# Moving the scatters of a second graph's edges between stages of a GNN and mixture-of-experts kernel

## The chip, the cores and the metric

The kernel runs on one core of a Trainium2 chip. It is one launch that computes eight stages. The metric is the device time of an execution in microseconds; the median of ten runs is given, and one profiled execution beside it. The engines are named as the profile names them: PE (TensorE, with PEld for its weight loads), DVE (VectorE), ACT (ScalarE), POOL (GpSimd) and SP (SyncE, which here issues most transfers). A name with a q behind it (SPq, POOLq) is the engine's sequencer.

## What is computed

Four graph rounds alternate with four mixtures of experts over 3125 nodes of 256 features; each reads the layer norm of x and adds its result to x.

```python
edge_index = jnp.stack([src, dst])                       # 50000 edges
x = x + _L0_gnn_ref(_layernorm(x), edge_weight, src, dst)        # round one: weighted sum over edges
x = x + _L0_ffn_ref(_layernorm(x), ...)                          # mixture one: top 2 of 8, relu, 512 hidden
x = x + _L1_gnn_ref(_layernorm(x), edge_index, ...)              # round two: two attention layers
x = x + _L1_ffn_ref(_layernorm(x), ...)                          # mixture two: top 2 of 8, gelu, 256 hidden
x = x + _L2_gnn_ref(_layernorm(x), edge_index, edge_weight, ...) # round three: normalised convolution
x = x + _L2_ffn_ref(_layernorm(x), ..., L2_ffn_edge_index)       # mixture three, routed by attention
x = x + _L3_gnn_ref(_layernorm(x), edge_index, ...)              # round four
x = x + _L3_ffn_ref(_layernorm(x), ...)                          # mixture four
```

Mixture three is the one that uses the other graph. Its routing scores come from an attention over 65536 edges of their own plus one loop per node:

```python
src = jnp.concatenate([edge_index[0], loops])
dst = jnp.concatenate([edge_index[1], loops])
e = leaky_relu(a_src[src] + a_dst[dst], 0.2)
ee = jnp.exp(e - segment_max(e, dst)[dst])
alpha = ee / (segment_sum(ee, dst)[dst] + 1e-16)
agg = segment_sum(h[src] * alpha[:, :, None], dst) + b_gat
```

To work on these edges in dense tiles, the kernel first sorts them by the block of 128 nodes that their destination lies in.

## The kernel before

The nodes are padded to 25 tiles of 128 (T = 25, P = 128), and x stays in SBUF as the tile X for the whole program.

**The other graph's scatters.** `own_places` computes for each of the 65536 edges a packed record (os_rec, 128 x 512) and the place in a DRAM table (os_at) at which it belongs. `own_send` (L1822) writes them: each call issues the next n of 512 columns, one indirect transfer on POOL for each (L1826), 128 records of one word. With no n it issues all that are left. Its second argument names an instruction that the scatters wait for; this only spreads them out in time. `settle` (L1836) reads one word of the table back, a transfer on SP that waits for the scatters issued so far; it stands ahead of each branch of the program. `own_load` (L1840) reads the finished table into SBUF (L1866, L1868) and decodes it (L1872 to L1885), and `own_order` (L1887, tiles oo_y and oo_h) sorts the edges of a block; both belong to round three.

The 512 are issued as follows: 21 in `rank_edges` (3 x 7) and 40 before the main loop of round one (5 x 8); 200 in its first 100 steps, two a step, and 12 in its last 25 (`src % 2`); 84 in the first mixture's 28 chunks (send=3); 36 in round two, at the end of its first layer (`tail`, 4 x 9); 98 in the second mixture's 28 chunks (send=3, more=2, thus 3 and 4 in turn); 21 at its end.

**Round one** (`r0_gnn`, L1482) runs 5 x 25 steps: five groups of destination tiles g, and in each all 25 source tiles. A step builds one-hot matrices on DVE (r_hs L1544, r_hd L1549), multiplies them on PE into a PSUM tile r_pw, copies that to SBUF on ACT (r_wt, L1557: the instruction `done` that a step's scatters wait for) and applies it to x on PE (L1521). Beside the steps of the first four groups the buckets of the next group are filled (`fill_bucket`: bf_h, bf_rh L1473, bf_hr, bf_ps on DVE, ACT and PE).

**Routing of a mixture.** In the last group of a round, as soon as five tiles of x are final, `mix_step` routes them: centred on ACT or DVE (gh_xn; ACT L191 in round one), squared, normalised, multiplied with the gate, top 2 picked on DVE, places computed (gd_at, L861). `mix_send` (L869) then scatters the ten batches (five tiles, two choices) from gh_xn on POOL into the DRAM regions of the experts. The tile gh_xn has two buffers. POOL, like each engine, runs what it is given in order, so L869 comes after all L1826 issued before it.

**The mixture** (`gated`) works in chunks of 256 rows of one expert: transfers in on SP (gx_xs, gx_w), transposes and two products on PE, the activation on ACT (gx_h, L1005; the last one of a chunk is what that chunk's scatters wait for), results out (ff_results). The next round begins with gathers of these results on POOL (gb_y, L360), which DVE adds to X (L1035).

**Round two** (`r1_gnn`) runs two attention layers. In each, POOL gathers rows for the edges (ad_rows, L360), and PE, DVE and ACT work on them. `tail` is called four times, twice in each of the last two blocks of the first layer; POOL has the last two calls' scatters just ahead of the second layer's first gathers.

The order of the instructions on each engine is set by a scheduler, except that from the first mixture to the second (`middle`, L2421) POOL's order is that of the text.

Of the kernel before, what the change touches and what calls it, by code (L numbers as in the profile page):

```python
# [27 lines left out]
AF = mybir.ActivationFunctionType  # L28
# [7 lines left out]
T = 25  # L36
# [27 lines left out]
class Net:  # L64
# [972 lines left out]
    def r0_ffn(self):  # L1037
        with ExitStack() as ctx:
            m = self.mix_whole(ctx, "L0_ffn_Wg", ("L0_ffn_bg", "L0_ffn_bias"), 8)
            self.sort_dst_end()  # L1040
            self.gated(m, "L0_ffn_W1", "L0_ffn_b1", "L0_ffn_W2", "L0_ffn_b2", AF.Relu)
# [20 lines left out]
    def r1_ffn(self):  # L1062
        with ExitStack() as ctx:
            m = self.mix_whole(ctx, "L1_ffn_router_w", (), 8, probs=True, transpose=True, add=True)
            self.gated(m, "L1_ffn_w1", "L1_ffn_b1", "L1_ffn_w2", "L1_ffn_b2", AF.Gelu)
# [149 lines left out]
class Fast(Net):  # L1215
# [266 lines left out]
    def r0_gnn(self):  # L1482
# [9 lines left out]
        G = 5  # L1492
        self.mix_way = ExitStack()
        m = self.mix = self.mix_start(self.mix_way, "L0_ffn_Wg", ("L0_ffn_bg", "L0_ffn_bias"), 8, act=True)
        with ExitStack() as ctx:
            pool = ctx.enter_context(tc.tile_pool(name="r0", bufs=1))
            lp = ctx.enter_context(tc.tile_pool(name="ln", bufs=1))
            bp = ctx.enter_context(tc.tile_pool(name="r0_b", bufs=2))
            hp = ctx.enter_context(tc.tile_pool(name="r0_h", bufs=3))
            psb = ctx.enter_context(tc.tile_pool(name="r0_pb", bufs=1, space=PSUM))  # L1500
            psw = ctx.enter_context(tc.tile_pool(name="r0_pw", bufs=2, space=PSUM))
            psa = ctx.enter_context(tc.tile_pool(name="r0_pa", bufs=2, space=PSUM))
            xn = pool.tile([P, T, D + 1], F32, name="r0_xn")
            nc.vector.memset(xn[:, :, D:], 1.0)
            iota1 = pool.tile([P, P], F32, name="r0_iota1")
            nc.vector.tensor_scalar_add(iota1, self.iota, 1.0)
            degs = pool.tile([P, T, T // G], F32, name="r0_degs")
            f5 = self.fill_fields(pool)
            for g in range(0, T, TG):
                self.norm_group(lp, xn[:, g:g + TG, 0:D], g, act=g // TG % 2 == 1)  # L1510

            wp = ctx.enter_context(tc.tile_pool(name="r0_w", bufs=2))

            psm = ctx.enter_context(tc.tile_pool(name="r0_pm", bufs=1, space=PSUM))
            self.mix_open(m, ctx, lambda: psb.tile([P, 512], F32, name="bf_ps"),
                          lambda: psm.tile([P, 80], F32, name="gh_ps"))

            def apply(g, src, wt):
                pa = psa.tile([P, D + 1], F32, name="r0_pa")
                for i in range(G):  # L1520
                    nc.tensor.matmul(pa, wt[:, i, :], xn[:, g * G + i, :], start=i == 0, stop=i == G - 1)  # L1521
                nc.vector.tensor_add(self.X[:, src, :], self.X[:, src, :], pa[:, 0:D])
                nc.scalar.copy(degs[:, src, g:g + 1], pa[:, D:D + 1])
                if g == T // G - 1:

                    self.mix_send(m, 2)
                    for _ in range(1 if src < T - 2 else 2):
                        self.mix_step(m, src + 1)


            for d in range(G):
                for _ in self.fill_bucket((bp, psb), f5, d):
                    pass
                self.own_send(8, self.filled)
            last = None
            for g in range(T // G):
                ds = slice(g * G, g * G + G)
                for src in range(T):
                    if g + 1 < T // G:
                        if src % G == 0:  # L1540
                            fill = self.fill_bucket((bp, psb), f5, (g + 1) * G + src // G)
                        next(fill, None)
                    hs = hp.tile([P, G, P], F32, name="r0_hs")
                    nc.vector.tensor_tensor(hs, self.iota[:, None, :].to_broadcast([P, G, P]),  # L1544
                                            s.bsrc[:, ds, src, None].to_broadcast([P, G, P]), OP.is_equal)
                    hd = hp.tile([P, G, P], F32, name="r0_hd")
                    for i in range(G):
                        d = g * G + i
                        nc.vector.tensor_scalar(hd[:, i, :], iota1, s.bdst[:, d, src:src + 1], s.bw[:, d, src:src + 1],  # L1549
                                                op0=OP.is_equal, op1=OP.mult)  # L1550
                    pw = psw.tile([P, G, P], F32, name="r0_pw")
                    for i in range(G):
                        nc.tensor.matmul(pw[:, i, :], hd[:, i, :], hs[:, i, :], start=True, stop=True)
                    if src % G == 0:
                        wide = wp.tile([P, G, G, P], F32, name="r0_wt")
                    wt = wide[:, src % G]
                    done = nc.scalar.copy(wt, pw)  # L1557
                    if src % G == G - 1:
                        nc.sync.dma_start(self.mats[:, src - G + 1:src + 1, ds, :], wide)
                    if last:  # L1560
                        apply(*last)
                    last = (g, src, wt)
                    self.own_send(2 if g < T // G - 1 else src % 2, done)
            apply(*last)
            self.mix_rest(m)
            nc.vector.tensor_reduce(self.deg, degs, AX.X, OP.add)
# [778 lines left out]
    def r1_gnn(self):  # L2345
# [5 lines left out]
        with tc.tile_pool(name="r1", bufs=1) as pool, tc.tile_pool(name="r1_ps", bufs=1, space=PSUM) as psp:  # L2351
# [38 lines left out]
                    self.mix_step(m, b + 1)  # L2390

            def tail(i):
                self.own_send(9, i)

            def rest(i):
                self.mix_send(m)

            self.attend(self.d, 64, rows[0], ad[0], sf[0], to_second, tail=tail)
            only.close()
            with ExitStack() as way:  # L2400
# [7 lines left out]


    def r0_ffn(self):  # L2410
        self.gated(self.mix, "L0_ffn_W1", "L0_ffn_b1", "L0_ffn_W2", "L0_ffn_b2", AF.Relu, beside=self.fill_edges, send=3, tail=False)

    def r1_ffn(self):
        self.gated(self.mix, "L1_ffn_w1", "L1_ffn_b1", "L1_ffn_w2", "L1_ffn_b2", AF.Gelu, send=3, more=2, tail=False)
        self.own_send()

    def r3_ffn(self):
# [415 lines left out]
```

## Time and profile before

| | us |
|---|---|
| median of ten runs | 5641.38 |
| lowest, highest | 5632.95, 5648.07 |
| the profiled execution | 5649.52 |
| its span | 5647.6 |
| PE busy | 3628.6 (64%) |
| DVE busy | 2849.8 (50%) |
| ACT busy | 2165.2 (38%) |
| POOL busy | 2107.0 (37%), 2107 instructions |

The stages in the span of the profiled execution, read from the first and last instructions of their own tiles, with the busy time in each:

| stage | from to | PE | DVE | ACT | POOL |
|---|---|---|---|---|---|
| setup, sorting of the first graph | 0-200 | 33.3 | 160.9 | 50.4 | 35.0 |
| round one, first group | 200-346 | 101.5 | 119.9 | 92.6 | 118.9 |
| round one, up to the last group | 346-608 | 261.8 | 219.5 | 159.1 | 152.8 |
| round one, last group, and routing | 608-778 | 126.5 | 112.7 | 70.8 | 62.7 |
| first mixture | 778-998 | 213.8 | 49.1 | 55.0 | 81.6 |
| round two | 998-2815 | 790.7 | 825.7 | 812.7 | 969.5 |
| second mixture | 2815-2998 | 135.7 | 42.6 | 28.4 | 95.8 |
| round three, its start | 2998-3104 | 27.0 | 57.8 | 11.1 | 85.4 |
| the rest | 3104-5647 | 1938.5 | 1261.7 | 885.1 | 505.4 |

A stage in which one engine is busy nearly all the time is bound by that engine; where none is, some wait sets the pace. In the lines of the profile, the bracket at the end of a timeline row gives the engine's idle time before the instruction and what ended it, and "issue" means that nothing in the profile held it.

### The profile page before, as it was taken

Reading aid. Unit: us, or ns where it says so; the run is one execution under the profiler, and the core shown is the slowest. Engines: PE = TensorE matmul, PEld = TensorE weight load, DVE = VectorE, ACT = ScalarE, POOL = GpSimd, SP = SyncE. Lnnn points to the kernel's source line nnn. Section 1 sums busy time; section 2 is a strip of 40 time slices with the busy share of each in tenths; the row PEclk is TensorE's granted clock in tenths of the full one; section 3 lists DMA queues with packets and bytes.
Section 4 is the critical chain, followed back from the end, with each engine's and each line's share of the span. In section 5 each row is a group of like instructions: output and inputs, shape, how many; then the busy total and the mean of one; then the engine's idle time right before and its main releaser. Section 6 shows DMA issues by size and latency. Waiting matters only on the chain. (4 is left out here: it accounts for less than half of the span.)

```text
span 5647.6 us, 66173 instructions
## 1 busy us (share of the span) xinstructions
PE 3628.6 (64%) x20909; PEld 2868.9 (51%) x20909; DVE 2849.8 (50%) x9396; ACT 2165.2 (38%) x5957; POOL 2107.0 (37%) x2107
## 2 busy tenths in 40 slices
PE   1499979324555324444583887554666699997994
PEld 1389868223333213333362776432433488886883
DVE  7978731434444325455524786524545788422112
ACT  2556432134554335445411797311222443111221
POOL 0765433555555455555357000255554000011003
PEclk9699979656666656666696998776887799997997
DMA  1722247333333133333162222201111011233554
GB/s 50 234 88 94 101 158 225 102 98 95 106 98 101 48 94 99 96 95 97 60 200 81 105 94 83 58 18 26 22 22 26 8 58 65 83 107 126 189 193 143
DMA packets 329438, 543.00 MB, mean 96 GB/s; under 512 B 69070, under 2 KB 242002, under 8 KB 325872
## 3 DMA queue, kind: packets, MB, share of 16 engines
q1 hardware_dynamic: 213430, 354.48, 18.6%
q0 software_dynamic: 84032, 154.27, 10.5%
q10 hardware_dynamic: 31610, 29.84, 1.6%
q8 instruction: 173, 2.83, 0.2%
q14 instruction: 193, 1.58, 0.1%
HBM read 393.49 MB, written 145.37 MB: 95 GB/s over the span
## 5 line engine op out<-in xcount | busy, mean ns | idle before, releaser
L360 POOL DMA_INDIRECT ad_rows<-r_rows,fa_gi x832 | 829.9, 997 | 614.8 <-PE ad_acc L2223 325.0
L1826 POOL DMA_INDIRECT os_table<-os_rec,os_at x512 | 548.7, 1072 | 631.3 <-ACT gx_h L1005 185.1
L360 POOL DMA_INDIRECT ad_rows<-q_rows,own_gi x416 | 400.3, 962 | 864.3 <-DVE ad_hb L2104 508.2
L2213 ACT ACTIVATE ad_rows<-ad_rows 128x64 f32<-128x64 f32 x2544 | 633.6, 335 | 90.7 <-issue 88.1
L2223 PE MATMUL ad_acc<-ad_rows,ad_hd 128*128 128x260 f32 x1664 | 601.9, 524 | 31.7 <-ACT ad_rows L2213 22.7
L2223 PEld LDWEIGHTS ad_acc<-ad_rows,ad_hd 128*128 128x128 f32 x1664 | 419.4, 266 | 121.6 <-ACT ad_rows L2213 29.0
L1654 PE MATMUL r_pa<-r_xs,r_cnt 128*128 128x257 bf16 (+1 forms) x3750 | 458.5, 276 | 9.2 <-issue 8.9
L869 POOL DMA_INDIRECT regions<-gh_xn,gd_at x150 | 148.1, 987 | 836.0 <-PE r_pa L1654 544.8
L1005 ACT ACTIVATE gx_h<-gx_pa,gx_bias 128x256 f32<-128x256 f32 x392 | 184.8, 473 | 603.5 <-PE gx_pa L1004 514.1
L1654 PEld LDWEIGHTS <-r_cnt 128*128 128x128 bf16 x3750 | 364.3, 99 | 64.3 <-issue 13.8
L974 PE MATMUL gx_po<-gx_w,gx_h 128*128 128x256 f32 x1568 | 374.7, 385 | 17.5 <-ACT gx_h L1005 14.1
L1004 PE MATMUL gx_pa<-gx_xt,gx_w 128*128 128x256 f32 x1568 | 370.6, 392 | 14.4 <-DVE gx_xt L999 8.7
L976 DVE TENSOR_TENSOR gx_ys<-gx_po,gx_b 128x256 f32<-128x256 f32 x168 | 70.8, 423 | 578.7 <-PE gx_po L974 495.0
L1004 PEld LDWEIGHTS gx_pa<-gx_xt,gx_w 128*128 128x128 f32 x1568 | 299.1, 195 | 80.3 <-DVE gx_xt L999 21.1
L360 POOL DMA_INDIRECT gb_y<-ff_results,gd_at x150 | 155.2, 1035 | 486.6 <-SPq L126 437.7
L2112 ACT CAST ad_hd<-ad_hb 128x2176 f32<-128x2176 bf16 (+1 forms) x50 | 98.3, 1967 | 608.8 <-PE ad_acc L2223 441.4
L974 PEld LDWEIGHTS gx_po<-gx_w,gx_h 128*128 128x128 f32 x1568 | 293.5, 193 | 60.3 <-ACT gx_h L1005 17.8
L2126 PE MATMUL ad_pt<-ident,ad_e 128*4 128x128 f32 x75 | 26.1, 348 | 453.1 <-DVE ad_F L2120 203.1
L1521 PE MATMUL r_pa<-r_xn,r_wt 128*128 128x257 f32 x1250 | 302.3, 387 | 19.8 <-ACT r_wt L1557 18.2
L2600 PE MATMUL ss_sum<-r_xw,ss_wt 128*128 128x256 f32 x1250 | 289.9, 394 | 6.2 <-DMA ss_wt<-mats 6.2
L2600 PEld LDWEIGHTS ss_sum<-r_xw,ss_wt 128*128 128x128 f32 x1250 | 245.4, 198 | 41.7 <-issue 6.6
L2182 PE MATMUL ad_px<-ad_nb,ad_hT 128*128 128x24 bf16 x1248 | 45.3, 179 | 333.2 <-DVE ad_nb L1420 234.8
(573 smaller groups left out, 7180.9 us busy)
## 6 DMA issues: line engine op xcount, KB each, us to landing
gx_w<-in_L_ffn_W SPq DMA_DIRECT2D x56, 1024.0 KB
mats<-r_wt SPq DMA_DIRECT2D x25, 1600.0 KB
ss_wt<-mats SPq DMA_DIRECT2D x25, 1600.0 KB
gx_w<-in_L_ffn_W SPq DMA_DIRECT2D x56, 512.0 KB
regions<-zero SPq DMA_DIRECT2D x26, 1024.0 KB
ad_rb<-fa_relT SPq DMA_DIRECT2D x48, 544.0 KB
gx_xs<-regions SPq DMA_DIRECT2D x84, 256.0 KB
ff_results<-gx_ys ACTq DMA_DIRECT2D x84, 256.0 KB
```

What stands on the lines that cost most here:

```text
L360: return self.nc.gpsimd.indirect_dma_start(out=out, out_offset=None, in_=table[:, :], in_offset=bass.IndirectOffsetOnAxis(ap=idx, axis=0))
L869: ins = nc.gpsimd.indirect_dma_start(out=self.regions[:, :], out_offset=bass.IndirectOffsetOnAxis(ap=m.at[i][:, t:t + 1], axis=0), in_=x, ...
L974: nc.tensor.matmul(po, h[:, f, j * P:(j + 1) * P], w2s[:, f, :], start=f == 0, stop=f == FC - 1)
L1004: nc.tensor.matmul(ps, w1s[:, c, f * P:(f + 1) * P], xt[:, c, :], start=c == 0, stop=c == DC - 1)
L1005: done = nc.scalar.activation(h[:, f, :], ps, act, bias=bias1[:, f, k:k + 1])
L1521: nc.tensor.matmul(pa, wt[:, i, :], xn[:, g * G + i, :], start=i == 0, stop=i == G - 1)
L1654: nc.tensor.matmul(pa[:, 0:n], c[:, u, :], xs[i][:, u, j, 0:n], start=u == 0 and j == 0, stop=u == T - 1 and j == 2)
L1826: i = nc.gpsimd.indirect_dma_start(out=s.table[:, :], out_offset=bass.IndirectOffsetOnAxis(ap=s.at[:, c:c + 1], axis=0), in_=s.rec[:, c, : ...
L2112: nc.scalar.copy(x.hd[:, :x.kb, :], x.hb[:, :x.kb, :])
L2213: i = nc.scalar.activation(v, v, AF.Copy, scale=x.rt[:, k, W4 + h:W4 + h + 1])
L2223: nc.tensor.matmul(x.acc, lhs[:, k, :], rhs[:, k, :], start=i == 0, stop=i == x.kb - 1)
L2600: nc.tensor.matmul(sums[t], wt[:, d, :], xw[:, d, :], start=d == 0, stop=d == T - 1)
```

## The change

Four numbers change. The scatters of the first 100 steps of round one go from two to three a step; `tail` issues 7 and not 9; the first mixture issues four a chunk and not three; the second mixture's calls ask for one a chunk, and find none left, and so does the call behind it.

```diff
@@ r0_gnn
-                    self.own_send(2 if g < T // G - 1 else src % 2, done)
+                    self.own_send(3 if g < T // G - 1 else src % 2, done)
@@ r1_gnn
             def tail(i):
-                self.own_send(9, i)
+                self.own_send(7, i)
@@ r0_ffn
-        self.gated(self.mix, "L0_ffn_W1", "L0_ffn_b1", "L0_ffn_W2", "L0_ffn_b2", AF.Relu, beside=self.fill_edges, send=3, tail=False)
+        self.gated(self.mix, "L0_ffn_W1", "L0_ffn_b1", "L0_ffn_W2", "L0_ffn_b2", AF.Relu, beside=self.fill_edges, send=4, tail=False)
@@ r1_ffn
-        self.gated(self.mix, "L1_ffn_w1", "L1_ffn_b1", "L1_ffn_w2", "L1_ffn_b2", AF.Gelu, send=3, more=2, tail=False)
+        self.gated(self.mix, "L1_ffn_w1", "L1_ffn_b1", "L1_ffn_w2", "L1_ffn_b2", AF.Gelu, send=1, tail=False)
         self.own_send()
```

| where | scatters before | after |
|---|---|---|
| `rank_edges` | 21 | 21 |
| round one, ahead of its steps | 40 | 40 |
| round one, first 100 steps | 200 | 300 |
| round one, last 25 steps | 12 | 12 |
| first mixture, 28 chunks | 84 | 112 |
| round two, four tails | 36 | 27 |
| second mixture, 28 chunks | 98 | 0 |
| behind it | 21 | 0 |

## The prediction

> **What bounds the kernel now.** I began with the page, whose engine rows show no engine full over the span, so the stages bound it one by one. Next came the group of the scatters (L1826), then windows of POOL with that line alone, then the timeline wherever a scatter stands ahead of something that others need. The columns of a window are its bounds, its length, busy time (instructions), TensorE's granted clock, DMA share and GB/s.
>
> ```profile
> L1826 POOL DMA_INDIRECT os_table<-os_rec,os_at x512 | 548.7, 1072 | 631.3 <-ACT gx_h L1005 185.1
> ...
> 300.00:346.00 46.00, 35.93 (x32) 0.94 0.19 63
> 346.00:608.00 262.00, 152.79 (x150) 1.00 0.26 93
> 778.00:994.00 216.00, 81.58 (x84) 0.99 0.72 225
> ```
>
> The mean is 1.07 us, and the pause to the next one 0.30, so back to back one takes 1.277 us where nothing stretches it. Round one has two regimes. Up to 345.7 POOL works off the 40 scatters of the prefill and never pauses: the 31 that start from 300.57 on take (345.7-300.57)/31 = 1.455 us each. After that, with two scatters in each step of 3.5 us, it idles (109 of 262 us). What bounds that stage is TensorE, busy 261.82 of the 262 us. The reason for 1.455 is in the timeline:
>
> ```profile
> 314.17 0.97 POOL L1826 DMA_INDIRECT os_table<-os_rec,os_at  x1 [0.30 <-issue]
> ...
> 315.15 2.37 DVE L1473 TENSOR_TENSOR bf_rh<-bf_h,bf_f 128x2125 bf16<-128x2125 bf16 x1 [4.73 <-PE r_pa L1521]
> ...
> 315.45 2.91 POOL L1826 DMA_INDIRECT os_table<-os_rec,os_at  x1 [0.30 <-ACT bu_dst L1479]
> ...
> 318.67 0.97 POOL L1826 DMA_INDIRECT os_table<-os_rec,os_at  x1 [0.30 <-issue]
> 318.90 1.10 DVE L1549 TENSOR_SCALAR r_hd<-r_iota,bu_dst,bu_w 128x128 f32<-128x128 f32 x4
> ```
>
> The scatter of 315.45 begins under a DVE tensor_tensor and ends 0.84 us after it (318.36 against 317.52); the one of 318.67 lies beside r_hd and keeps its 0.97. So a scatter is stretched by some DVE operations, not by all. The rows that decide the rest follow: POOL and ACT in the first mixture's routing, then the boundary of the second layer of round two, then the start of round three.
>
> ```profile
> 659.42 0.97 POOL L869 DMA_INDIRECT regions<-gh_xn,gd_at  x1 [0.84 <-DVE gd_at L861]
> ...
> 671.47 0.97 POOL L869 DMA_INDIRECT regions<-gh_xn,gd_at  x1 [0.30 <-issue]
> ...
> 675.88 2.10 ACT L191 ACTIVATE gh_xn<-X,ln_m 128x256 f32<-128x256 f32 x5
> ...
> 754.09 0.51 ACT L191 ACTIVATE gh_xn<-X,ln_m 128x256 f32<-128x256 f32 x1 [4.07 <-DMA regions<-gh_xn,gd_at]
> ```
>
> ```profile
> 1948.26 0.97 POOL L1826 DMA_INDIRECT os_table<-os_rec,os_at  x1 [0.30 <-issue]
> 1949.54 0.98 POOL L360 DMA_INDIRECT ad_rows<-r_rows,fa_gi  x1 [0.30 <-issue]
> ```
>
> ```profile
> 2997.38 0.98 POOL L360 DMA_INDIRECT gb_y<-ff_results,gd_at  x1 [3.71 <-SPq L126]
> ...
> 3002.43 1.00 POOL L1826 DMA_INDIRECT os_table<-os_rec,os_at  x1 [0.30 <-issue]
> ...
> 3028.03 0.97 POOL L1826 DMA_INDIRECT os_table<-os_rec,os_at  x1 [0.30 <-issue]
> 3029.31 0.98 POOL L360 DMA_INDIRECT gb_y<-ff_results,gd_at  x1 [0.30 <-issue]
> ...
> 3032.33 0.48 DVE L1035 SCALAR_TENSOR_TENSOR X<-gb_y,gd_w,X 128x256 f32<-128x256 f32 x1 [25.05 <-DMA gb_y<-ff_results,gd_at]
> ```
>
> The tile gh_xn has two buffers. ACT's write of the third group (675.88) reuses the one that the first ten L869 scatters read, so it waits until they have landed; the row at 754.09 shows that wait in the open. At the start of round three 21 leftover scatters stand between the fourth and the fifth gather, and DVE waits 25.05 us.
>
> **The change, part by part.** It counts as follows: 21 + 40 + 300 + 12 + 28x4 = 485 by the end of the first mixture, then tails of 7, 7, 7 and 6 make 512. The second mixture's 98 and the final 21 go to nothing.
>
> *Round one (L1563).* Three scatters need 3x1.277 = 3.83 us or more in a step of 3.5, so POOL no longer catches up. Ahead of the first L869 scatter stand 347 instead of 247; 90 are done at 345.7, which leaves 257. At 1.455 us POOL has worked off (678-345.7)/1.455 = 228 of them when ACT comes to the third group's write at 676 to 678. ACT then waits, in order, and behind it stand the copies of pw to SBUF (L1557, each step), the degree copies and the square of the norm; TensorE waits for L1557 and DVE for both, and with DVE quiet the other 29 run at 1.277: the first L869 at 678+36.5 = 714.5 instead of 659.42. The ten take 12.4 us, land 1.3 later, and ACT answers 0.1 after: the third group's write is late by 714.5+13.8-675.9 = 52.4. All that follows in round one and the first mixture hangs on it; what PE and DVE may have run ahead by then I put at 2. **+50.** Bounds: 1.277 throughout gives the first L869 at 673.9, net +9.8; the mean of all 90 unbroken ones, (345.4-197.17)/90 = 1.647, until the wait gives 748.5, net +84. I take 1.455, the row of the same loop's own steps; the 59 before it lie beside five bucket fills in a row. If ACT's wait had cover (a third buffer), the 50 would go.
>
> The Trainium skill speaks against this part: "GPSIMD Engine Reference" (1. Specifications) has GpSimd's SBUF interfaces shared with VectorE, with contention for instructions in a two-port mode or with two SBUF inputs. The trace bears out the two-input half (2.91 us at 315.45) and leaves r_hd's rows undisturbed. Read as the trace has it, the rule gives the +50; without any sharing the part would be worth +9.8.
>
> *First mixture (send 4).* A chunk takes 7.53 us (28 in some 211 us; TensorE is busy 213.75 of the 220 from 778 to 998), four scatters 5.1: hidden beside TensorE. They move 128 words each. After the last chunk the results transfer (issued 994.26, landed 996.24) ends later than the fourth scatter (some 994.4). **0**, and +1.3 if the scatter came last.
>
> *Tails of round two (9 to 7).* At the boundary there were 18 scatters directly ahead of the second layer's first gather (1949.54), whose rows had landed at 1936.7; now there are 13. 5x1.28: **-6.4.** The 33.3 us that DVE waits for these gathers show that they are on the path; if not, 0.
>
> *Something that the text of the change doesn't show.* With the final scatters gone from the queue, the loads of the binned table (L1866) and the operations that decode it move ahead, out of the start of round three into the last routing step of round two. There DVE's L1872 stands ahead of L821 of the routing softmax (2789.60) and waits for a transfer that took 3.84 us (3030.18 to 3034.02); ten decode operations (some 3 us by their rows of 3109 to 3122) and ACT's 17 oo_y (0.3 each in round three, partly beside) stand in between. **+6.5**, bounds 3 and 8.
>
> *Second mixture.* No scatters beside it: its chunks average 5.95 us with waits for ACT and DVE, 3 or 4 scatters no longer in POOL's queue: **-1** (bounds -4, +2). At its end the table's mark was the last to land (scatter to 2993.68, mark 2994.87, gather 2997.38). Now the results decide (issued 2990.74); by the first mixture's end, 4.33 us from that issue to the gather, the gather starts at 2995.07: **-2.3.**
>
> *Start of round three.* From 3002.43 to 3029.31 POOL runs leftovers and nothing else moves (TensorE 0.00 busy from 2998 to 3030): **-26.9.** Gathers follow each other at 1.26 us as before. The decode, 4.5 us of DVE, and the first block's 7 us of ACT are no longer at this start, where half lay beside POOL's additions: **-3.5** (0 to -5).
>
> Sum: 50 + 0 - 6.4 + 6.5 - 1 - 2.3 - 26.9 - 3.5 = **+16.4**. The profiled run took 5649.5 (span 5647.6, 1.9 around it), so its changed twin takes 5666; it lies 8.1 above the median of the ten runs, and on the median the sum gives **5658 us**.
>
> **Rivals.**
> - *Faster: scatters keep near 1.277 in round one.* The price of the part is then +9.8 and the time 5641.4-23.8 = 5618. For: 150 scatters of the second regime average 152.79/150 = 1.02. Against: those start just after ACT's copy, in a quiet spot of the step, which a full queue can't choose. The sign turns at 1.375 us each, a 0.2% gain is reached under 1.327.
> - *About the same: the stretch ends with the fills.* After 605 the bucket fills (L1473) are over. At 1.455 to 605 and 1.277 from there, 235 are done at 678, the first L869 comes at 705.6, net +41.5, in all +7.9: 5649. For: the longest stretches come from the fills. Against: r_hs stays in each step, and the routing brings DVE operations of two inputs.
> - *Heavier: the prefill's 1.647 holds.* +84 in place of 50: 5692. Against: its 59 first scatters lie beside denser work.
> - *The change doesn't empty the later stages.* The count of 485+27 = 512 excludes it.
>
> **How the numbers follow.** Forecast 0.58, heavier 0.10, same 0.16, faster 0.16. The likeliest's own range is 5646 to 5670: hoist 3 to 8, start 0 to -5, mixture -4 to +2, and 8 for round one. To leave out no more than 2 in 10, it goes down into the faster case, to 5632, and up to 5676. A measurement of this kernel can tell about 0.2% (11 us) from no change: faster 0.16, same 0.16, slower 0.68.
>
> **What would show it.** The first L869 near 714 instead of 659; ACT's L191 of the third group with an idle time near 50 us, released by regions; the first mixture's first chunk 50 later than 778.4; thirteen scatters, then the gather, near 6 us earlier relative to its surroundings; gathers of gb_y in one row; L1872 in the last routing step waiting for fa_rec. The prediction falls if scatters in round one take under 1.375 each, if TensorE goes on working while ACT waits, or if round three's start was held by something else than POOL.

## The result and the profile after

The change made the kernel slower by more than was forecast: 5690.26 us median (5682.81 to 5695.46, 8 runs) against 5642.16 (5624.95 to 5663.32, 28 runs), a ratio of 1.0083 with a 95% interval of 1.0072 to 1.0094. That is +48 us; the forecast was +17 (5658, range 5632 to 5676). In the experiments below one execution of e10 (8226.59 us) and one of e15 (7678.16 us) fell into a slow state; the ratios leave them out, but the medians listed for these two runs include them.

The profiled execution took 5681.57 us, 9 below its median, and its span is 5679.8 against 5647.6. The pair of profiles is thus 32.2 apart. Followed from landmark to landmark in both traces, the difference comes about like this:

| from, to | before | after | difference | forecast |
|---|---|---|---|---|
| r_wt copy of step 0 to that of step 25 | 107.4 | 141.5 | +34.1 | 0 |
| step 25 to step 100 | 262.5 | 346.0 | +83.5 | 0 |
| step 100 to the first mixture's first chunk | 169.5 | 171.1 | +1.6 | +50 |
| first mixture, first to last chunk | 204.6 | 208.0 | +3.4 | 0 |
| tails (to the second layer's first gather) | | | -12.2 | -6.4 |
| last routing of round two (to its L927) | | | +3.3 | +6.5 |
| the rest of round two | | | -8 | 0 |
| second mixture, first chunk to the first gather behind it | 177.6 | 141.2 | -36.4 | -3.3 |
| the leftovers in front of the fifth gather | | | -26.0 | -26.9 |
| start of round three | | | -2.2 | -3.5 |
| all that follows | | | -9 | 0 |

The rows of -8 and -9 have no explanation here; single executions of the kernel before lie up to 38 us apart.

The wait that the prediction was built on is not there. POOL's first scatter of the routing and ACT's write of the third group, in the timeline of the changed kernel:

```profile
777.24 0.97 POOL L869 DMA_INDIRECT regions<-gh_xn,gd_at  x1 [0.85 <-DVE gd_at L861]
...
793.69 2.10 ACT L191 ACTIVATE gh_xn<-X,ln_m 128x256 f32<-128x256 f32 x5
```

L869 starts 0.85 us after DVE has computed its places, as before (0.84): POOL's queue was not behind. It could keep up because the steps had become slower. Windows of all engines over the 75 steps behind the first group, before and after (the columns are PE, PEld, DVE, ACT and POOL busy, then clock, DMA share, GB/s):

```profile
346.00:608.00 262.00, 261.82 (x1739) 238.47 (x1738) 219.47 (x567) 159.09 (x452) 152.79 (x150) 1.00 0.26 93
```

```profile
381.00:727.00 346.00, 295.29 (x1746) 256.06 (x1745) 222.03 (x571) 159.62 (x454) 245.87 (x226) 0.93 0.21 71
```

The same instructions of TensorE take 84 us longer: it is busy 33 us longer, and it now has 51 us of pauses. How they look is seen in the timeline of the changed kernel, at two of the first 25 steps, where they are longest (in the 75 they last up to 5.2 us):

```profile
253.85 1.28 PE L1553 MATMUL r_pw<-r_hs,r_hd 128*128 128x128 f32 x10
...
259.74 0.69 ACT L1557 COPY r_wt<-r_pw 128x640 f32<-128x640 f32 x1 [6.37 <-remote]
...
264.65 0.83 PE L1553 MATMUL r_pw<-r_hs,r_hd 128*128 128x128 f32 x6
...
266.06 0.27 PE L1553 MATMUL r_pw<-r_hs,r_hd 128*128 128x128 f32 x1 [0.58 <-issue]
...
268.85 0.37 PE L1553 MATMUL r_pw<-r_hs,r_hd 128*128 128x128 f32 x1 [2.52 <-issue]
...
270.27 0.57 PE L1553 MATMUL r_pw<-r_hs,r_hd 128*128 128x128 f32 x1 [1.05 <-issue]
...
273.06 0.37 PE L1553 MATMUL r_pw<-r_hs,r_hd 128*128 128x128 f32 x1 [2.22 <-issue]
...
275.76 0.97 POOL L1826 DMA_INDIRECT os_table<-os_rec,os_at  x1 [0.31 <-issue]
277.04 0.97 POOL L1826 DMA_INDIRECT os_table<-os_rec,os_at  x1 [0.30 <-issue]
277.27 0.42 DVE L1522 TENSOR_TENSOR X<-X,r_pa 128x256 f32<-128x256 f32 x1 [16.70 <-remote]
...
277.72 0.16 ACT L1523 COPY r_degs<-r_pa 128x1 f32<-128x1 f32 x1 [14.60 <-issue]
```

At 264.65 six matmuls of a step start 0.11 us apart, as they should. The seventh starts 0.86 us after the sixth, and the last three 1.4 to 2.8 us after one another, with "issue" in the bracket: nothing that the profile shows holds them. Elsewhere such starts lie 0.7 us apart. DVE and ACT, which wait for TensorE's products, idle for 16.70 and 14.60 us, while POOL prepares one scatter after the other with the usual 0.30 between them. Such a stretch comes every 10 to 40 us, inside POOL's unbroken runs of scatters. I call it the slow stretch.

Over the 75 steps only some 21 us of the 51 are marked "issue"; 29 the profile puts down to ACT's r_wt. But that copy waits for TensorE in turn: at 259.74 it starts 4.6 us after the recorded end of the matmuls that it reads (253.85 + 1.28). So the delay is on TensorE's side, and the recorded ends don't show all of it.

The granted clock falls in these stretches too. Two windows with the columns as above:

```profile
265.00:267.50 2.50, 0.75 (x6) 0.52 (x5) 0.00 (x0) 0.00 (x0) 1.89 (x3) 1.00 1.00 312
268.00:291.00 23.00, 4.41 (x10) 3.09 (x10) 5.54 (x16) 4.00 (x12) 13.94 (x15) 0.50 0.54 175
```

The first window has the first pause, at the clock of 1.00; the clock falls at 267.8. All 14 falls of the clock from 250 to 727 us come 2 to 9 us after the first pause of their stretch. So the lower clock may add to the loss, but it doesn't begin the pauses.

The other side of the change behaved: in round two 13 scatters and then the gather, and in round three the gathers of gb_y with nothing between them.

```profile
2061.82 0.97 POOL L1826 DMA_INDIRECT os_table<-os_rec,os_at  x1 [0.30 <-issue]
2063.09 0.98 POOL L360 DMA_INDIRECT ad_rows<-r_rows,fa_gi  x1 [0.30 <-issue]
```

```profile
3067.01 0.98 POOL L360 DMA_INDIRECT gb_y<-ff_results,gd_at  x1 [151.38 <-SPq L126]
3068.30 0.96 POOL L360 DMA_INDIRECT gb_y<-ff_results,gd_at  x1 [0.30 <-issue]
```

### The profile page after: what moved, and what is told of

Read it like the earlier page. It is cut to its first block, busy times and chain, and to the rows that moved or that the text cites. A ratio compares the mean times of both kernels' runs of the same rounds, so it can differ in the third digit from the quotient of the medians.

```text
span 5679.8 us, 66143 instructions
## 1 busy us (share of the span) xinstructions
PE 3653.3 (64%) x20909; PEld 2883.7 (51%) x20909; DVE 2852.5 (50%) x9396; ACT 2164.4 (38%) x5957; POOL 2123.0 (37%) x2107
## 3 DMA queue, kind: packets, MB, share of 16 engines
q0 software_dynamic: 84032, 154.27, 10.5%
## 5 line engine op out<-in xcount | busy, mean ns | idle before, releaser
L1826 POOL DMA_INDIRECT os_table<-os_rec,os_at x512 | 563.1, 1100 | 516.0 <-issue 140.9
L869 POOL DMA_INDIRECT regions<-gh_xn,gd_at x150 | 148.0, 987 | 838.3 <-PE r_pa L1654 545.5
L1521 PE MATMUL r_pa<-r_xn,r_wt 128*128 128x257 f32 x1250 | 326.1, 408 | 63.0 <-ACT r_wt L1557 58.7
L1521 PEld LDWEIGHTS r_pa<-r_xn,r_wt 128*128 128x128 f32 x1250 | 242.9, 204 | 106.2 <-ACT r_wt L1557 65.8
```

The source lines that it names most:

```text
L869: ins = nc.gpsimd.indirect_dma_start(out=self.regions[:, :], out_offset=bass.IndirectOffsetOnAxis(ap=m.at[i][:, t:t + 1], axis=0), in_=x, ...
L1826: i = nc.gpsimd.indirect_dma_start(out=s.table[:, :], out_offset=bass.IndirectOffsetOnAxis(ap=s.at[:, c:c + 1], axis=0), in_=s.rec[:, c, : ...
```

## The experiments

Two theories stood against each other. Theory S: TensorE slows while POOL prepares scatters without a pause. Theory L, the prediction's: the steps keep their pace, and a late L869 makes ACT wait. Each job ran the kernel before on its own chip too, and the chips differ (5639 to 5700 us for the kernel before on most of them, 4865 and 4867 on two, told apart below as slowing chips and chips that don't slow), so ratios are compared, and the times inside a trace. "Steps" is the time from step 0 to step 25 and from there to step 100; "second" is the second mixture from its first to its last chunk.

| run | median, before on the same chip | ratio (95%) | steps | second |
|---|---|---|---|---|
| e1 | 5757.79, 5700.50 | 1.0103 (1.0086 to 1.0120) | 142.3 + 357.6 | 139.8 |
| e2 | 5661.12, 5700.50 | 0.9933 (0.9917 to 0.9950) | 116.9 + 264.1 | 159.9 |
| e3 | 5674.43, 5700.50 | 0.9950 (0.9933 to 0.9967) | 128.6 + 298.9 | 136.0 |
| e4 | 5721.57, 5700.50 | 1.0041 (1.0027 to 1.0056) | 117.6 + 291.7 | 165.8 |
| e5 | 5805.86, 5681.84 | 1.0221 (1.0201 to 1.0241) | 140.4 + 348.1 | 164.2 |
| e6 | 5719.77, 5681.84 | 1.0081 (1.0052 to 1.0110) | 99.3 + 294.6 | 169.3 |
| e7 | 5743.27, 5681.84 | 1.0107 (1.0090 to 1.0124) | 115.2 + 262.9 | 129.3 |
| e8 | 5772.69, 5681.84 | 1.0160 (1.0143 to 1.0177) | 92.7 + 262.8 | 131.9 |
| e9 | 4833.55, 4866.98 | 0.9931 (0.9918 to 0.9944) | 96.1 + 261.2 | 133.4 |
| e10 | 4834.28, 4866.98 | 0.9930 (0.9917 to 0.9943) | 94.9 + 261.2 | 135.9 |
| e11 | 5688.71, 5638.65 | 1.0087 (1.0064 to 1.0110) | 106.6 + 380.0 | 131.8 |
| e12 | 5759.55, 5638.65 | 1.0210 (1.0172 to 1.0249) | 143.1 + 346.4 | 159.4 |
| e13 | 5613.55, 5641.22 | 0.9949 (0.9934 to 0.9965) | 108.0 + 262.7 | 162.5 |
| e14 | 5623.44, 5641.22 | 0.9969 (0.9956 to 0.9981) | 99.9 + 262.5 | 181.7 |
| e15 | 5694.57, 5641.22 | 1.0088 (1.0068 to 1.0108) | 142.4 + 348.8 | 131.8 |
| e16 | 4883.82, 4865.48 | 1.0035 (1.0019 to 1.0051) | 95.6 + 261.1 | 130.9 |

**e1 and e2: the change taken apart.** e1 is the kernel before with the third scatter in round one alone. e2 is the changed kernel with two a step again, and the 99 that this leaves beside and behind the second mixture.

```diff
 e1, against the kernel before
-                    self.own_send(2 if g < T // G - 1 else src % 2, done)
+                    self.own_send(3 if g < T // G - 1 else src % 2, done)
 e2, against the changed kernel
-                    self.own_send(3 if g < T // G - 1 else src % 2, done)
+                    self.own_send(2 if g < T // G - 1 else src % 2, done)
-  ... "L1_ffn_b2", AF.Gelu, send=1, tail=False)
+  ... "L1_ffn_b2", AF.Gelu, send=3, more=2, tail=False)
```

> Only the third scatter a step in round one; everything else as before, so 19 scatters are left for the second mixture and none behind it. Theory S (TensorE's instructions come slowly, some 0.7 us apart, as long as POOL runs scatters without a pause): the first 100 steps end about 118 us later, as in the changed kernel; the second mixture gains about 28, the leftovers 27, so 5642 + 118 - 28 - 27 - 3 = about 5700. Theory L (the prediction's: the steps keep their pace and ACT waits about 50 us for a late L869): steps end at about 608, then a wait of 50; about 5655.

> The changed kernel with two scatters a step in round one again; the 99 left go beside the second mixture (98) and behind it (1). Theory S: round one as before; tails -12; the second mixture about as slow as before (180 us, not 147); leftovers -25: about 5642 - 37 = 5605. Theory L: tails -6, leftovers -25, second mixture as in the changed kernel only if its gain there had another cause than the scatters (then about 147 us and 5575).

On one chip, e1's 100 steps take 119 us more than e2's, and e1 is 1.0103 of the kernel before; e2 is 0.9933. Theory S foresaw both within a few us, theory L's 5655 for e1 falls. So the change without its third scatter of a step (e2) gains some 39 us. The third scatter costs 119 us in the steps, and it empties the second mixture, which gives back some 28. The second mixture shows the same effect from its other side: 160 us with 98 scatters beside it (e2), 136 with 51 (e3), 132 with none (the changed kernel).

**e3: 2 and 3 in turn.**

```diff
 against the changed kernel
-                    self.own_send(3 if g < T // G - 1 else src % 2, done)
+                    self.own_send(2 + src % 2 if g < T // G - 1 else src % 2, done)
-  ... "L1_ffn_b2", AF.Gelu, send=1, tail=False)
+  ... "L1_ffn_b2", AF.Gelu, send=2, tail=False)
```

> The changed kernel with 2 and 3 scatters in turn in round one (248 in 100 steps) and 51 beside the second mixture, two a chunk. POOL needs 2.48 x 1.28 = 3.2 us a step of 3.5 unstretched, some 3.6 stretched. Theory S: the loss follows the time that POOL has no pause, so between 20 and 90 us of the 118. A theory of a price per scatter (count alone): 48 of 100 extra scatters, 57 us. Theory L: POOL nearly keeps up, the first L869 at most 15 us late, no loss before it.

The 100 steps take 46.5 us more than e2's on the same chip, for 48 extra scatters where 100 cost 119. That lies in theory S's range, but the price for each scatter is nearly the same (0.97 and 1.19 us), so e3 doesn't tell S from a plain price for each.

**e4: is it POOL being full?** A third instruction in each step occupies POOL without any transfer.

```diff
 against the kernel before
                     self.own_send(2 if g < T // G - 1 else src % 2, done)
+                    if g < T // G - 1:
+                        fi = nc.gpsimd.iota(busy, pattern=[[1, 1024]], ...)
+                        tc.add_manual_dep(fi.ins, done.ins.name, ...)
```

> The kernel before, with an iota of 1024 words on POOL (about 1 us, no transfer, a tile that nothing reads) beside the two scatters of each of the first 100 steps, so that POOL is as full as in the changed kernel. If the full queue of POOL itself slows TensorE: the steps end some 100 us later, 5740. If it is the scatters' own descriptors and transfers: steps end at 608 to 615, and at most the late L869 is left (0 to +50): 5642 to 5690 with TensorE's pace in the steps unchanged.

The same columns for e4's 75 steps, and a row of its timeline:

```profile
356.00:648.00 292.00, 273.26 (x1748) 242.16 (x1748) 287.84 (x572) 158.19 (x455) 256.28 (x225) 1.00 0.24 85
```

```profile
481.51 2.62 DVE L1551 TENSOR_SCALAR r_hd<-r_iota,bu_dst,bu_w 128x128 f32<-128x128 f32 x5
```

POOL is busier than in the changed kernel (256.28 of 292 us, and no pause over 0.6 us in the whole stretch), and no slow stretch of TensorE is left in these steps: none of its pauses is an "issue", they are all waits for r_wt or r_hs of 1.3 us at most, and the clock stays at 1.00. The steps still lose 27.6 us, by something else that I had not foreseen: five r_hd take 2.62 us where 1.36 is usual, DVE is busy 287.84 of 292 us and becomes the bound. A full POOL alone does not make the slow stretches: with an iota behind every two scatters, so that no more than two stand in a row, they are gone.

**e5 and e12: is it what the scatters write?** The third transfer of each step aims outside the table, so that no record is placed.

```diff
 against the kernel before
                     self.own_send(2 if g < T // G - 1 else src % 2, done)
+                    if g < T // G - 1:
+                        fi = nc.gpsimd.indirect_dma_start(out=o.table[:, :],
+                            out_offset=bass.IndirectOffsetOnAxis(ap=far[:, 0:1], axis=0),
+                            in_=o.rec[:, 0, :], bounds_check=OS - 1, oob_is_err=False, ...)
```

> The kernel before, with a third indirect transfer in each of the first 100 steps whose 128 places all lie outside the table, so that POOL prepares a scatter and nothing of it is written. If the transfers' own writes slow TensorE: no slow stretches, the 75 steps after the first group stay near 262 to 275 us. If preparing scatters without a pause slows it: the 75 steps take 340 to 360 us, as with the third real scatter, and the first 25 some 140.

> The run e5_oob once more (the kernel before and 100 scatters whose places all lie outside the table). Where TensorE slows: 1.02. Where it doesn't: steps at 262 us, the first L869 some 50 late, the last group and the routing longer by that, 1.010 to 1.013.

The 75 steps of e5:

```profile
379.00:727.00 348.00, 299.51 (x1763) 260.92 (x1763) 223.40 (x573) 160.12 (x455) 246.23 (x225) 0.92 0.21 73
```

The row is that of the changed kernel again, to a few us, and on two chips. Records of the third scatter that land in the table are not the cause. The transfers themselves are not excluded: the queue of these transfers shows 87232 packets against 84032, so each of the 100 still moved 32 packets, as a placed scatter does.

**e6: the same scatters, bunched.** Ten behind every fifth step, same number and mean rate as before.

```diff
 against the kernel before
-                    self.own_send(2 if g < T // G - 1 else src % 2, done)
+                    self.own_send((10 if src % G == G - 1 else 0) if g < T // G - 1 else src % 2, done)
```

> The kernel before with the same 200 scatters in the first 100 steps, but ten behind every fifth step and not two behind each. Same number and same mean rate; POOL runs some 12.8 us without a pause and rests some 4.7. If the length of a run without a pause is what counts: TensorE loses some us in each run, 15 runs after the first group, 30 to 90 us in all. If only the mean rate or the count counts: the 75 steps take 262 to 270 us as before.

The 75 steps of e6:

```profile
338.00:633.00 295.00, 273.40 (x1748) 243.67 (x1748) 219.58 (x569) 157.80 (x456) 160.47 (x150) 0.99 0.24 85
```

The 75 steps take 294.6 us where two a step take 262.5 to 264.1: 30 to 32 us for the same 150 scatters. The length of a run counts, and a theory of a fixed price for each scatter falls.

**e7 and e8: room in round two?** e7 puts 127 scatters between the gathers of round two and none into the tails, the second mixture or behind it; e8 puts the 40 of the prefill there too.

```diff
 against e2
+                if j == 1 and x.b < T - 2 and getattr(self, "spread", 0):
+                    self.own_send(self.spread)
...
-                self.own_send(7, i)
+                self.own_send(0, i)
+            self.spread = 3                 # e8: 4, and own_send(0) in the prefill
-  ... "L1_ffn_b2", AF.Gelu, send=3, more=2, tail=False)
+  ... "L1_ffn_b2", AF.Gelu, send=1, tail=False)
```

> Round one with two a step as before, four a chunk in the first mixture, none in the tails, the second mixture and behind it; the other 127 go between the gathers of round two, three behind the first third of a block's weighting (blocks 0 to 22 of the first layer, then of the second). POOL idles some 9 us of the 30.7 of a block, three scatters take 3.8. If that idle time is free: tails -46, second mixture -30, leftovers -27, hoisted table +4, first mixture +3: about 0.983 of the time before. If gathers are what round two waits for: +127 x 1.28 = 163 us of it comes back, 1.012.

> As the run before, but the 40 scatters ahead of round one's steps go to round two too, four a block in both layers. Theory S (scatters without a pause slow TensorE): the first 25 steps, 107 to 117 us with the 40, come down towards 25 x 3.5 = 88; some 20 us less than the run before, if round two hides four a block as well as three. Without that effect: the same as the run before.

Both are slower than the kernel before: POOL's idle 9 us a block is not free. Against e2's trace, e7 falls behind by some 90 us over the first layer's 69 scatters, 1.3 us each, the full price of a scatter. But e8's first 25 steps take 92.7 us in place of e7's 115.2: without the prefill POOL has pauses there, and the steps come near their 3.5 us, as theory S has it.

**e9, e10, e13, e14: shorter runs in the mixtures.** e9 is e2 with a chunk's scatters shared out over its activations; e10 adds less prefill, none in the tails, five and four a chunk. e13 and e14 are the same two on another chip.

```diff
 e9, against e2
                             done = nc.scalar.activation(h[:, f, :], ps, act, bias=bias1[:, f, k:k + 1])
-                        if send and k < KA:
-                            self.own_send(send + k % more, done)
+                            if send and k < KA:
+                                n = send + k % more
+                                self.own_send((f + 1) * n // FC - f * n // FC, done)
 e10, against e9: own_send(8 -> 5, self.filled), own_send(7 -> 0, i), send=4 -> 5 in r0_ffn, send=4 in r1_ffn
```

> The run e2_r0_back with the same number of scatters in each chunk of the mixtures, but one or two behind each activation and not all behind the chunk's last (first mixture 1, 1, 1, 1; second 1 and 2, or 2 and 2). Theory S, in the form that the length of a run without a pause counts: second mixture from 160 us to 135 to 145, first mixture some 2 to 5 us shorter; 0.989 to 0.991 of the time before where e2_r0_back had 0.9933. If only number or mean rate counts: both mixtures as in e2_r0_back, 0.993.

> All that was found together: 25 scatters ahead of round one's steps and not 40, two a step, five a chunk in the first mixture and four in the second, split over the activations; none in the tails; two left behind the second mixture. Theory S: first 25 steps some 92 to 100 us and not 107 to 117 (-10 to -20), tails -46, second mixture between 135 and 160 (-25 to 0), leftovers -24, first mixture up to 10 longer, hoisted table 0 to +4: 0.982 to 0.989 of the time before. If five scatters a chunk keep POOL without a pause in the first mixture, that stage grows by 20 and more, and the sum comes to 0.99.

> As e9_split. On a chip where TensorE slows: second mixture 135 to 145 us and not 160, 0.989 to 0.991 of the time before. Without an effect of the length of a run: 0.993, as e2_r0_back.

> As e10_combined. On a chip where TensorE slows: first 25 steps 92 to 100 us and not 107 to 117, tails -46, leftovers -24, second mixture between 135 and 160: 0.982 to 0.989 of the time before.

e9 and e10 met a chip on which the kernel before takes 4867 us, and there is no slow stretch in round one's steps at all. The second mixture with its 98 scatters, on that chip (e9) and on a slowing one (e13):

```profile
2331.00:2470.00 139.00, 121.81 (x560) 93.06 (x560) 40.80 (x84) 27.75 (x57) 93.17 (x96) 0.97 0.77 234
```

```profile
2812.00:2980.00 168.00, 132.60 (x560) 101.44 (x560) 40.81 (x84) 27.36 (x57) 93.11 (x96) 0.91 0.65 193
```

Same instructions and same POOL work, 133.4 us against 162.5 from first to last chunk: where TensorE does not slow, 98 scatters beside that mixture cost next to nothing (130.9 without any, e16), and e10's 112, which POOL works off there in one unbroken run, take the mixture to 135.9. On the slowing chip e13 won nothing (162.5, e2 159.9) where I had expected 135 to 145. But its edit did not shorten the runs. POOL in e13's second mixture:

```profile
2882.19 0.97 POOL L1827 DMA_INDIRECT os_table<-os_rec,os_at  x1 [3.18 <-ACT gx_h L1005]
...
2889.85 0.97 POOL L1827 DMA_INDIRECT os_table<-os_rec,os_at  x1 [0.30 <-issue]
```

Seven scatters stand in a row here, 0.30 us apart. In e13 as in e2 the scatters beside this mixture come in some 20 runs, nine of them of seven scatters and none longer. So e13 does not test the length of a run. In this mixture the length of the runs and the share of the time that POOL needs rise together, and nothing separates them: 51 scatters of 1.28 us (e3) need 49% of the 132 us, come in runs of one or two and cost 4 us; 98 need 95%, come in runs of up to seven and cost 28; e14's 112 need 109%, come in runs of up to twelve and cost 50. In the first mixture e14's five a chunk make 226.2 us of 204.6. e14 gave back in the two mixtures what it gained elsewhere. All four ratios, 0.9930 to 0.9969, miss what was expected of shorter runs (0.982 to 0.991).

**e11, e15, e16: the changed kernel on other chips.**

> The changed kernel once more, beside the kernel before on the same chip. Theory S on a chip where TensorE slows beside scatters without a pause (before takes 5640 to 5700): 1.007 to 1.010, the 75 steps after the first group some 346 us. On a chip where TensorE shows no such slow stretches (before took 4867 there), the steps can't slow: they keep 262 us, and theory L is left alone: the first L869 late, ACT's wait of some 50 us behind it, tails and leftovers -35 and no gain in the second mixture: 1.002 to 1.006.

> The changed kernel. On a chip where TensorE slows: 1.007 to 1.010. On one where it doesn't: steps at 262 us, first L869 late by some 50, tails and leftovers -35, second mixture as before: 1.002 to 1.006.

> The changed kernel. On a chip where TensorE slows: 1.007 to 1.010. On one where it doesn't (before at 4867): steps at 262 us, first L869 late by some 50, 1.002 to 1.006.

On two further slowing chips the result repeats, 1.0087 and 1.0088. In e11 the loss lies elsewhere in the steps than expected: the first 25 take 106.6 us, as in the kernel before, and the 75 take 380.0, not 346. e16 met a chip without slow stretches, and there the prediction's mechanism stands in the open. Windows of the 75 steps and of the last group, then the timeline:

```profile
335.00:596.00 261.00, 261.00 (x1745) 238.90 (x1744) 224.55 (x571) 159.81 (x454) 206.84 (x178) 1.00 0.27 95
596.00:760.00 164.00, 96.61 (x592) 86.13 (x591) 82.33 (x318) 53.74 (x116) 113.11 (x113) 0.80 0.19 64
```

```profile
707.30 0.97 POOL L869 DMA_INDIRECT regions<-gh_xn,gd_at  x1 [0.30 <-issue]
...
721.36 2.10 ACT L191 ACTIVATE gh_xn<-X,ln_m 128x256 f32<-128x256 f32 x5 [64.17 <-DMA regions<-gh_xn,gd_at]
```

TensorE is busy all 261 us beside a full POOL. The first L869 is held by nothing but the queue in front of it (forecast 714.5, measured 707.30), ACT idles 64.17 us for the ten scatters to land, and the last group ends 58.3 us later than e9's (759.9 against 701.6; forecast +52.4, less 2), whose round one is that of the kernel before. The whole change costs 18.3 us there; the forecast was 16.4. That it came so near is in part luck: round one cost 8 more than forecast, and the rest gave back some 40 where 33.6 was forecast.

**The best version** that was measured against the kernel before is e2, and e9 and e13, which are e2 with the chunks' scatters shared out: 0.9931 to 0.9949 on three chips, thus some 0.5% to 0.7% faster than the kernel before and faster than the changed one on both kinds of chip.

## Why the prediction was wrong

The sign and the place, round one, were right; the mechanism was not, on the chip of the result, so the sign was right by luck.

*Round one.* The step that failed is "At 1.455 us POOL has worked off (678-345.7)/1.455 = 228 of them when ACT comes to the third group's write": it takes for granted that the steps keep 3.5 us beside a POOL without pauses. On the chips that slow they took 4.6 (346.0/75), POOL was done in time, and the forecast wait of 50 us was replaced by a loss of 117.6 in the steps. e4, e5 and e6 put that loss on unbroken runs of indirect transfers. On a chip without slow stretches (e16) the step holds: 58.3 measured for 50.

*Second mixture.* "3 or 4 scatters no longer in POOL's queue: -1" was mis-sized for the same reason: with the better end of the mixture -3.3 was forecast, and -36.4 came. The irregular chunks of the kernel before (3.7 to 10.7 us) were put down to ACT and DVE waits. Without scatters the changed kernel's chunks take 3.7 to 6.2 us, and with them e9's 3.7 to 6.1 on its chip and e13's 3.7 to 10.4 on a slowing one: the long chunks go where the slow stretches go. The two errors have opposite signs and hid a part of each other.

*Tails.* The mechanism held, the number was 5 of 9 scatters: the first pair of tails is on the path as well, and 9 x 1.28 = 11.5 is near the 12.2 measured.

*Hoisted table.* The decode did move into the last routing step and cost +3.3. The 3.84 us wait of DVE did not appear: the load had been issued at 2877.6, some 14 us ahead of L1872.

*Leftovers and start of round three.* -26.0 and -2.2 for -26.9 and -3.5: right.

*Rivals.* The faster one, scatters near 1.277 us, falls: in e16 POOL works off 178 of them in 261 us, 1.466 each, where 1.455 was forecast; in the 75 steps of the changed kernel on the chip of the result they took 245.87/226 + 0.30 = 1.39 with the gap, and its time was not that rival's. The one in which the stretch ends with the fills put the first L869 at 705.6, which looks nearer to e16's 707.30 than the forecast's 714.5. But e16's step 100 comes at 595.8 and that of the kernel before at 608.9. Counted from there the first L869 comes after 111.5 us, where the forecast has 105.6 and this rival 96.7, so it falls too, and the forecast was 6 short. None of the rivals named a slower TensorE. The trace of before did show one, in round four, where POOL issues ten L869 scatters without a pause (timeline of the kernel before):

```profile
4978.97 0.97 POOL L869 DMA_INDIRECT regions<-gh_xn,gd_at  x1 [0.31 <-issue]
...
4981.23 0.60 PE L1654 MATMUL r_pa<-r_xs,r_cnt 128*128 128x256 bf16 x4 [0.82 <-issue]
...
4982.66 0.50 PE L1654 MATMUL r_pa<-r_xs,r_cnt 128*128 128x256 bf16 x3 [0.83 <-issue]
4982.80 0.97 POOL L869 DMA_INDIRECT regions<-gh_xn,gd_at  x1 [0.30 <-issue]
...
4984.79 2.52 PE L1654 MATMUL r_pa<-r_xs,r_cnt 128*128 128x256 bf16 x12 [1.14 <-issue]
```

TensorE's "issue" pauses begin inside the batch, and end 1 us after its last scatter (4982.80 + 0.97). In the same way the first 25 steps took 107.4 us beside the prefill where 25 x 3.5 = 88 would do; on e9's chip they take 96.1, so some 11 of these 19 us belong to the slow stretches. Both could be read ahead of the prediction.

## What to carry to other kernels

An engine that is off the path can slow the one on it without any semaphore between them: before filling an idle queue, look in the trace for a place where it is already full and compare the busy engine's pace there with its pace elsewhere. "issue" in front of the instructions of an engine that is the bound is such a sign. Leave POOL pauses when it prepares transfers beside TensorE work: in this kernel, on the slowing chips, two scatters in 3.5 us were free, and two and a half were not.

## What the runs showed of the hardware

**Chips differ by 14% on this kernel.** The kernel before takes 5639 to 5700 us on the slowing chips, and 4865 and 4867 us on the two others. The two have no slow stretches in round one; round two, with its 832 gathers prepared by POOL, takes 1367 us from the end of the first mixture to the second in e9 and 1825 in e13, the same kernel. A ratio measured on one kind of chip need not hold on the other: the change costs 0.83% to 0.88% on the first kind and 0.35% on the second. Each of the six chips of the experiments was met in one job only, so chip and job are not told apart, and why the two kinds differ is open.

**What makes TensorE slow is not settled.** It needs indirect transfers that POOL prepares, in unbroken runs (e6 against two a step); a POOL filled with something else does not do it (e4), and records landing in the table are not needed (e5). The Trainium skill ("Runtime: NRT & Kernel Launch", Instruction fetch mechanics) states that an engine's instructions are streamed in blocks of 16 KiB by transfers that are mostly hidden. Blocks of that size are in the trace, 173 packets of 16384 B on an instruction queue in each run. They took a median of 1.03 us in the kernel before and 0.98 in the changed one, both on slowing chips, and 0.97 in e9 and 1.00 in e16, so slow blocks are not what tells the chips apart. From 256 to 290 us the changed kernel's trace has none of them, so the stretch of 265 to 288 did not end with the arrival of one; whether fetching plays a part in another way was not tried. Each execution on record carries a recorded span and clock, and whether the recording plays a part was not tried either.

**An iota on POOL slows DVE where a scatter does not.** Beside the 1 us iota of e4 five r_hd took 2.62 us in place of 1.36, a tensor_scalar with one large input; over the 75 steps one took 0.78 us on average, against 0.36 before. Beside scatters they keep their time (0.37 in the changed kernel). The Trainium skill ("GPSIMD Engine Reference", 1. Specifications) names two-port modes and two SBUF inputs as the cases of contention. The second is the one that stretched the scatters before; the first may be the one seen here, and no run separates it.
